# Four-layer graph network on one core: layer 1's blocks, the token order, and the inputs of layers 0 and 2

## The chip, the core and the metric

The kernel runs on one core of a Trainium2 chip. A core has five engines that run side by side, each through its own list of instructions in order: TensorE (PE) multiplies matrices, VectorE (DVE) and ScalarE (ACT) work element by element, GpSimd (POOL) does the same and also issues the indirect transfers (gathers and scatters by index), and SyncE (SP) issues most other transfers. They wait for each other through semaphores. Matmul results land in PSUM, which has eight banks; everything else is in SBUF (on chip) or in DRAM. The metric is the device time of one execution in microseconds (us); lower is better.

## What is computed

The input is 3125 nodes with 256 features each, in fp32, and 50,000 edges. Four layers follow. Each normalises the rows, adds a graph part and a mixing part, and adds an expert or feed-forward part. What matters here:

```python
# every layer (layer 3 differs in details)
xn = _layernorm(x)
x = x + gnn(xn, edges) + mix(xn)
x = x + ffn(_layernorm(x))
# layer 0's ffn: 8 experts, all applied to all nodes, weighted with softmax(x @ Wr + br)
# layer 1's ffn: a shared expert (256 -> 1024 -> 256, gelu) for all nodes, and
#   8 routed experts (256 -> 1024 -> 256, gelu): each node takes its two best
# layer 3's graph part runs a scan over the nodes in this order:
perm = jnp.argsort(deg + deg_noise, stable=True)
```

`deg` counts a node's outgoing edges and `deg_noise` is an input, so layer 3's order depends on the inputs alone and can be found at any earlier time.

## The kernel before

The nodes lie in 25 tiles of 125 partitions (P = 125, NT = 25); `GROUPS` are six groups of four tiles and one of one. The residual X stays in SBUF through all four layers. The program text gives each operation once, in Python loops; a scheduler decides at build time in which order each engine's list holds them, from their dependences and from the pools (a pool is a region of SBUF or PSUM; a tile of a later pool may lie where an earlier pool's tiles lay, and then has to wait for them). At run time every engine keeps to its list.

Helpers. `evac` (L74) copies a PSUM result to SBUF, by VectorE (L78) and ScalarE (L80) in turn. `turn` (L144) transposes tiles on TensorE into the layout that matmuls need. `hidden` (L540) and `outward` (L553) are the two matrix products of an expert. `halves` (L778) splits a transfer in two. `layer_input` (L521) goes through the seven groups: for each tile the statistics (bn_stats L125, bn_aggr L126), a few small operations for 1/sqrt(variance), the normalised tile XN (L138), and its transposes into XNT.

Layer 0's experts, `l0_ffn` (L783): the layer's input; then `probabilities` (the router: 100 matmuls of eight columns, and a softmax); then for each of eight experts and seven groups two hidden products and one outward product, whose results VectorE adds into X with the node's weight (L825). In expert 1 the folded output biases are added tile by tile (`expert_bias`). One pool of seven PSUM banks serves all of this, and the layer's input has a pool of four banks (`li_ps`) that is opened and closed inside `layer_input`. Just before it comes layer 0's graph aggregation (agg, L759), 1250 matmuls with the adjacency read from DRAM, with X accumulated at its end.

Layer 1 starts in `layer1` (L1548), which first fills 8000 rows of DRAM (`f_rows`, 8 MB) with zeros, in eight transfers of 1 MB on the queues of SyncE and ScalarE in turn (`blank`, L1537). Its experts, `l1_ffn` (L1392): the input; the router; `l1_route`, which sorts the node and expert pairs so that each expert's nodes fill blocks of 250 rows (BLK), with `put[k]` the row of each node's k-th pair, `share[k]` its weight, and `owner[b]` the expert of block b. MAXB = 32 blocks is the number that can never be exceeded: 2 x 3125 pairs and up to 249 empty rows for each of eight experts. GpSimd scatters the nodes into `f_rows`, the shared expert runs, and then the loop over all 32 blocks. `load(b)` (L1436) reads a block's rows and its expert's 2 MB of weights on SyncE's queue, one block ahead, with three buffers. The block is turned (xbt), goes through `hidden` (hb, eight chunks, gelu on ScalarE) and `outward`, its two halves are copied to yb by VectorE and ScalarE in turn, and two transfers on ScalarE's queue write them to `f_out` in DRAM (L780, L781).

After the loop comes `l3_order` (L1872), which finds layer 3's order: `places` (L1684) spreads the keys of all nodes into every partition (25 transposes on TensorE, seven evacuations to place_row), and then counts on VectorE, tile by tile, how many keys are below each node's own (L1702): for tile i one tally over the i tiles before it (place_t), one over its own tile (place_e), and one over the tiles from i on (place_t), 74 in all. They read place_row and a mask of ones. A reduction (L1708) and a cast (L1881) give the order.

Then 50 gathers (`gather`, L2083, GpSimd) fetch each node's two rows from `f_out` to yg (six buffers, in the pool f1_k of the block loop), and VectorE adds each to X with its share (L1469). Layer 2 opens with `layer_input` (`layer2`, L1751), whose XN and XNT lie where layer 1's pools lay; the projection of layer 2's graph part puts h2 (h22, al22) beside h in the pool g2_h.

Of the kernel before, what the change touches and what calls it, by code (L numbers as in the profile page):

```python
# [12 lines left out]
F32 = mybir.dt.float32  # L13
BF16 = mybir.dt.bfloat16
I32 = mybir.dt.int32
# [3 lines left out]
PSUM = bass.MemoryType.PSUM  # L19
# [33 lines left out]
FMAX = 3.4028234663852886e38  # L53
BLK = 2 * P
MAXB = (2 * N + 8 * (BLK - 1)) // BLK
CAP = 489
GROUPS = [(g, min(4, NT - g)) for g in range(0, NT, 4)]
COLUMNS = [(0, 7), (7, 6), (13, 6), (19, 6)]
# [2 lines left out]
class Net:  # L61
# [456 lines left out]

    def layer_input(self, pool=None, xn=None, xnt=None):  # L521

        if pool is not None:
            xn = pool.tile([P, NT, D], F32, name="XN")
            xnt = pool.tile([128, KC, N], F32, name="XNT")
        with self.pool("li", 2) as wp, self.pool("li_ps", 4, PSUM) as pp:
            for g, n in GROUPS:
                self.normed(wp, xn[:, g:g + n, :], self.X[:, g:g + n, :], n, 1e-5, "li")
                self.turn(pp, xnt[:, :, g * P:(g + n) * P], xn[:, g:g + n, :], n)
        return xn, xnt  # L530
# [249 lines left out]
        queue.dma_start(out[:EVEN], in_[:EVEN])  # L780
        queue.dma_start(out[EVEN:], in_[EVEN:])  # L781

    def l0_ffn(self):  # L783
        nc = self.nc
        pre = "L0_ffn_"
        with ExitStack() as es:
            sp = es.enter_context(self.pool("f0"))
            xn, xnt = self.layer_input(sp)
            wp = es.enter_context(self.pool("f0_w", 2))
            kp = es.enter_context(self.pool("f0_k", 2))  # L790
            pp = es.enter_context(self.pool("f0_ps", 7, PSUM))
            wr = self.weight(sp, pre + "Wr")
            br = self.rows(sp, pre + "br")
            prob = self.probabilities(sp, pp, xnt, wr, br)
            more = self.expert_bias(sp, pp, prob, pre + "bo")
            scale, bias = [], []
            for k in ("1", "2"):
                b, g, be, m, v = (self.cols(sp, pre + t + k) for t in ("b", "g", "be", "m", "v"))
                s = sp.tile(list(v.shape), F32, name="bn_s" + k)
                nc.vector.tensor_scalar(v, v, 1e-3, None, op0=ALU.add)  # L800
                self.rsqrt(sp, s, v, "bn" + k)
                nc.vector.tensor_mul(s, s, g)
                nc.vector.tensor_sub(b, b, m)
                nc.vector.tensor_mul(b, b, s)
                nc.vector.tensor_add(b, b, be)
                scale.append(s)
                bias.append(b)
            mp = es.enter_context(self.pool("f0_m", 2))
            for e in range(8):
                w1 = self.weight(wp, pre + "W1", view=self.ins[pre + "W1"][e])  # L810
                w2 = self.weight(wp, pre + "W2", view=self.ins[pre + "W2"][e])
                wo = self.weight(wp, pre + "Wo", view=self.ins[pre + "Wo"][e])
                ce = slice(e * KC, (e + 1) * KC)
                for g, n in GROUPS:
                    w = n * P
                    h1 = kp.tile([128, KC, 4 * P], F32, name="h1")
                    h2 = kp.tile([128, KC, 4 * P], F32, name="h2")
                    self.hidden(pp, h1[:, :, :w], w1, [xnt[:, c, g * P:g * P + w] for c in range(KC)],
                                KC, AF.Relu, bias[0][:, ce], scale[0][:, ce])
                    self.hidden(pp, h2[:, :, :w], w2, [h1[:, c, :w] for c in range(KC)],  # L820
                                KC, AF.Relu, bias[1][:, ce], scale[1][:, ce])

                    def use(j, ps):
                        x = self.X[:, g + j, :]
                        nc.vector.scalar_tensor_tensor(x, ps, prob[:, g + j, e:e + 1], x,  # L825
                                                       op0=ALU.mult, op1=ALU.add)
                    self.outward(pp, h2, wo, KC, n, use)
                    if e == 1:
                        for _ in range(n):
                            next(more)  # L830
                    if g % 8 == 0 and e * 4 + g // 8 < NT:
                        self.mask_row(mp, e * 4 + g // 8)

    def layer0(self):
        with self.under_way:
            fill = self.fill_adjacency()
            for k, _ in enumerate(self.l0_mix(self.xnt0)):
                for _ in range(2 if k % 4 else 1):
                    next(fill, None)
            self.through(fill)  # L840
            self.sums.close()
            with self.pool("g0_h") as hp:
                h = self.l0_gnn_project(hp, self.xnt0)
                left = self.nc.values_load(self.left[0:1, 0:1], min_val=0, max_val=1)
                with self.tc.If(left > 0):
                    self.any_adjacency()
                self.l0_gnn(h)
        self.l0_ffn()

# [540 lines left out]
    def l1_ffn(self):  # L1392

        nc = self.nc
        pre = "L1_ffn_"
        with ExitStack() as es:
            sp = es.enter_context(self.pool("f1"))
            put = [sp.tile([P, NT], I32, name=f"put{k}") for k in range(2)]  # L1400
            share = [sp.tile([P, NT], F32, name=f"share{k}") for k in range(2)]
            owner = sp.tile([P, MAXB], I32, name="owner")
            rows = self.rows1
            out = self.dram.tile([MAXB * BLK, D], F32, name="f1_out")
            wp = es.enter_context(self.pool("f1_w", 3))
            kp = es.enter_context(self.pool("f1_k", 2))
            with ExitStack() as es2:
# [8 lines left out]
                nc.gpsimd.tensor_add(self.X, self.X, b2s[:, None, :].to_broadcast([P, NT, D]))  # L1416
                prob = self.probabilities(ip, pp, xnt, wr)
                rank = self.ranks(ip, prob)
                self.l1_route(ip, pp, prob, rank, put, share, owner)
                self.apart([self.scatter(rows, put[k][:, i:i + 1], xn[:, i, :]) for i in range(NT)  # L1420
                            for k in range(2)], "all pairs' rows differ")
                more = self.expert_bias(ip, pp, prob, pre + "b2p")
# [23 lines left out]
                nc.sync.dma_start(b1, self.ins[pre + "b1p"][bass.ds(e, 1)].rearrange("o p f -> p (o f)"))  # L1446
                return x, w1, w2, b1

            ahead = load(0)
            for b in range(MAXB):  # L1450
                (x, w1, w2, b1), ahead = ahead, load(b + 1) if b + 1 < MAXB else None
                xt = kp.tile([128, KC, BLK], F32, name="xbt")
                self.turn(pp, xt, x, 2)
                h = kp.tile([128, 8, BLK], F32, name="hb")
                self.hidden(pp, h, w1, [xt[:, c, :] for c in range(KC)], 8, AF.Gelu, b1)
                y = kp.tile([P, 2, D], F32, name="yb")

                def keep(j, ps):
                    self.evac(y[:, j, :], ps)
                self.outward(pp, h, w2, 8, 2, keep)  # L1460
                self.halves(nc.scalar, out[b * BLK:(b + 1) * BLK, :].rearrange("(j p) d -> p j d", p=P), y)

            self.l3_order(pp)
            for i in range(NT):
                for k in range(2):
                    y = kp.tile([P, D], F32, name="yg", bufs=6)
                    self.gather(y, out, put[k][:, i:i + 1])
                    x = self.X[:, i, :]
                    nc.vector.scalar_tensor_tensor(x, y, share[k][:, i:i + 1], x, op0=ALU.mult, op1=ALU.add)  # L1469

    def l1_route(self, pool, psum, prob, rank, put, share, owner):


        nc = self.nc
# [44 lines left out]
        nc.vector.tensor_reduce(number, past, axis=AX.X, op=ALU.add)  # L1519
        nc.vector.tensor_scalar(number, number, 7.0, None, op0=ALU.min)  # L1520
        nc.vector.tensor_copy(owner, number)

        nc.vector.tensor_add(off[:, :NT, :], off[:, :NT, :],
                             within[:P, :NT * 8].rearrange("p (i e) -> p i e", e=8))
# [9 lines left out]
            nc.vector.tensor_mul(t, prob, chosen)  # L1534
            nc.vector.tensor_reduce(share[k], t, axis=AX.X, op=ALU.add)

    def blank(self, rows, count):  # L1537

        nc = self.nc
        with self.pool("blank") as zp:  # L1540
            width = count * D // 128
            zero = zp.tile([128, width // 8], F32, name="zero")
            nc.gpsimd.memset(zero, 0.0)
            zv = rows.rearrange("r d -> (r d)").rearrange("(b p f) -> b p f", b=8, p=128)
            for b in range(8):
                (nc.sync, nc.scalar)[b % 2].dma_start(zv[b], zero)

    def layer1(self):  # L1548
        self.rows1 = self.dram.tile([MAXB * BLK, D], F32, name="f1_rows")
        self.blank(self.rows1, MAXB * BLK)  # L1550
        with self.pool("g1_h") as hp:
            with self.pool("in1") as ip:
                xn, xnt = self.layer_input(ip)
# [119 lines left out]
                nc.gpsimd.tensor_add(self.X[:, g:g + n, :], self.X[:, g:g + n, :], y[:, :n, :])  # L1673
        return h

    def l2_gnn_project(self, pool, xnt):
        h2 = pool.tile([P, NT, 1, D + 1], F32, name="h22")
        al2 = pool.tile([P, NT, 2], F32, name="al22")
        return self.gat_project(pool, xnt, "L2_gnn_", "W1", 4, ("a_src1", "a_dst1"), "g2") + (h2, al2)

    def l2_gnn(self, h):
# [67 lines left out]
                self.outward(pp, h, w2, 8, n, use)  # L1749

    def layer2(self):  # L1751
        with self.pool("g2_h") as hp:
            with self.pool("in2") as ip:
                xn, xnt = self.layer_input(ip)
                h = self.l2_mix(xn, xnt, lambda: self.l2_gnn_project(hp, xnt))
            self.l2_gnn(h)
        self.l2_ffn()

# [690 lines left out]
```

## Time and profile before

| what | us |
|---|---|
| median of 3 runs | 7255.4 |
| the runs | 7255.02, 7258.82, 7255.40 |
| the profiled execution | 7258.78 |
| its span, first to last instruction | 7257.0 |
| TensorE busy | 6018.7 (83%) |
| VectorE busy | 3847.7 (53%) |
| ScalarE busy | 1528.9 (21%) |
| GpSimd busy | 980.6 (14%) |
| layer 1's block loop: 1024 + 1024 matmuls | 227.5 + 226.2 |

The mean granted clock of TensorE is 0.889 of full speed (PEclk in the windows is the same figure for a stretch of time). Times in the rows of the profile count from the start of the span. A row of the groups has the line of the kernel, the engine, the operation, output<-inputs by name, the shapes and how often; then the busy time, the mean duration and the idle time before, with the event that ended it. A row of the order of time has start and duration in us, and in brackets how long the engine stood idle before it and what released it. The busy shares are means over stages of very different kinds, so a stage has to be read by its own window.

### The profile page before, as it was taken

Reading aid. Unit: us, or ns where it says so; the run is one execution under the profiler, and the core shown is the slowest. Engines: PE = TensorE matmul, PEld = TensorE weight load, DVE = VectorE, ACT = ScalarE, POOL = GpSimd, SP = SyncE. Lnnn points to the kernel's source line nnn. Section 1 sums busy time; section 2 is a strip of 40 time slices with the busy share of each in tenths; the row PEclk is TensorE's granted clock in tenths of the full one; section 3 lists DMA queues with packets and bytes.
Section 4 is the critical chain, followed back from the end, with each engine's and each line's share of the span. In section 5 each row is a group of like instructions: output and inputs, shape, how many; then the busy total and the mean of one; then the engine's idle time right before and its main releaser. Section 6 shows DMA issues by size and latency. Waiting matters only on the chain. (4 is left out here: it accounts for less than half of the span.)

```text
span 7257.0 us, 79169 instructions
## 1 busy us (share of the span) xinstructions
PE 6018.7 (83%) x29841; PEld 4048.7 (56%) x29841; DVE 3847.7 (53%) x7861; ACT 1528.9 (21%) x3255; POOL 980.6 (14%) x730
## 2 busy tenths in 40 slices
PE   6887999995999897999816998988788879985584
PEld 5555874554999786678714344875444343333452
DVE  7643223128666644110276887456377878776504
ACT  1333012331001100222213011001366640012110
POOL 0000000004000011300141000111244440002302
PEclk8877998997999998989957998989799979997697
DMA  2523457101221142245310222421300012220131
GB/s 65 105 50 65 136 160 235 35 5 61 60 60 56 51 133 84 75 135 179 117 36 23 79 75 66 136 73 31 56 12 17 9 43 82 69 59 21 39 127 56
DMA packets 407126, 540.56 MB, mean 74 GB/s; under 512 B 116440, under 2 KB 292187, under 8 KB 402939
## 3 DMA queue, kind: packets, MB, share of 16 engines
q1 hardware_dynamic: 355276, 462.70, 23.1%
q10 hardware_dynamic: 24664, 45.08, 2.0%
q0 software_dynamic: 26752, 27.19, 1.4%
q8 instruction: 248, 4.06, 0.2%
q14 instruction: 186, 1.52, 0.1%
HBM read 425.19 MB, written 109.43 MB: 74 GB/s over the span
## 5 line engine op out<-in xcount | busy, mean ns | idle before, releaser
L1109 DVE SCALAR_TENSOR_TENSOR t<-rows,over,a 125x625 f32<-125x625 f32 x750 | 621.9, 871 | 411.6 <-PE acc L1114 410.9
L1175 DVE SCALAR_TENSOR_TENSOR t<-rows,over,a 125x750 f32<-125x750 f32 (+1 forms) x800 | 795.4, 1045 | 57.6 <-PE acc L1189 53.1
L1180 PE MATMUL acc<-t,g_h 125*64 125x375 f32 (+1 forms) x3200 | 626.0, 501 | 12.8 <-DVE t L1175 12.8
L1114 PE MATMUL acc<-g_h,t 125*125 125x129 f32 x5000 | 568.5, 276 | 1.3 <-DVE t L1109 1.1
L1114 PE MATMUL acc<-h,t 125*125 125x257 f32 x2500 | 557.7, 386 | 13.8 <-DVE share_r L1221 7.1
L1114 PEld LDWEIGHTS acc<-g_h,t 125*125 125x125 f32 x5000 | 565.8, 190 | 2.7 <-DVE t L1109 2.7
L1114 PEld LDWEIGHTS acc<-h,t 125*125 125x125 f32 x2500 | 474.9, 191 | 95.6 <-issue 9.4
L1180 PEld LDWEIGHTS acc<-t,g_h 125*64 125x64 f32 x3200 | 227.6, 137 | 356.2 <-issue 246.3
L1189 PE MATMUL acc<-t,g_h 125*32 125x375 f32 (+1 forms) x3200 | 377.1, 497 | 0.0
L2030 POOL TENSOR_TENSOR bx<-h,crow 128x500 f32<-128x500 f32 (+1 forms) x224 | 265.6, 1201 | 388.8 <-DVE h L2027 278.9
L149 PE MATMUL ps_turn<-ident,XN 125*128 125x125 f32 x350 | 76.7, 390 | 287.0 <-DVE XN L138 244.8
L825 DVE SCALAR_TENSOR_TENSOR X<-ps_out,prob,X 125x256 f32<-125x256 f32 x200 | 87.8, 479 | 397.6 <-PE ps_out L156 397.5
L759 PE MATMUL agg<-h,a 125*125 125x257 f32 x1250 | 278.6, 384 | 15.3 <-DMA a<-adj 9.1
L2036 PE MATMUL y<-bx,ident 128*128 128x500 f32 (+1 forms) x448 | 234.1, 633 | 48.2 <-POOL bx L2030 46.6
L759 PEld LDWEIGHTS agg<-h,a 125*125 125x125 f32 x1250 | 234.6, 189 | 59.4 <-issue 17.3
L2027 DVE TENSOR_TENSOR_SCAN h<-da,state,bx 128x500 f32<-128x500 f32 (+1 forms) x224 | 246.8, 1131 | 11.7 <-ACT da L2025 8.4
L78 DVE COPY yb<-ps_out 125x256 f32<-125x256 f32 x32 | 13.6, 424 | 446.6 <-issue 394.3
L1189 PEld LDWEIGHTS acc<-t,g_h 125*32 125x32 f32 x3200 | 104.2, 109 | 249.2 <-issue 248.4
L156 PE MATMUL ps_hidden<-xbt,w 128*128 128x250 f32 x1024 | 227.5, 380 | 14.5 <-DVE xbt L78 14.4
L551 ACT ACTIVATE h<-ps_hidden,L_ffn_b,bn_s 128x500 f32<-128x500 f32 (+1 forms) x224 | 160.7, 722 | 373.2 <-PE ps_hidden L156 365.6
L149 PEld LDWEIGHTS ps_turn<-ident,XN 125*128 125x128 f32 x350 | 60.2, 203 | 302.4 <-issue 263.7
L156 PE MATMUL ps_out<-w,hb 128*125 128x256 f32 x1024 | 226.2, 379 | 0.0
(723 smaller groups left out, 10048.3 us busy)
## 6 DMA issues: line engine op xcount, KB each, us to landing
a<-adj SPq DMA_DIRECT2D x500, 273.4 KB
a<-adj SPq DMA_DIRECT2D x150, 328.1 KB
arow<-adj SPq DMA_DIRECT2D x25, 1367.2 KB
adj<-block SPq DMA_DIRECT2D x22, 1531.2 KB
w<-in_L_ffn_W1p SPq DMA_DIRECT2D x32, 1024.0 KB
w<-in_L_ffn_W2p SPq DMA_DIRECT2D x32, 1024.0 KB
a<-adj SPq DMA_DIRECT2D x50, 382.8 KB
L_ffn_w<-in_L_ffn_w SPq DMA_DIRECT2D x18, 1024.0 KB
```

Source lines behind the costliest of these rows:

```text
L149: self.nc.tensor.transpose(ps[:, j * P:(j + 1) * P], x[:, j, c * 128:(c + 1) * 128], self.ident[:P, :P])
L156: self.nc.tensor.matmul(ps, lhsT[k], rhs[k], start=(k == 0), stop=(k == n - 1))
L551: self.nc.scalar.activation(out[:, f, :], ps[:, :nt], func, **kw)
L759: nc.tensor.matmul(acc[b][:P, :D + 1], a[:, b * P:(b + 1) * P], h[:, s, :], start=(s == 0), stop=(s == NT - 1))
L1109: nc.vector.scalar_tensor_tensor(t[:, hd, :], rows[:, hd, :], over[:, s, hd:hd + 1], a, op0=ALU.max, op1=ALU.mult)
L1114: nc.tensor.matmul(acc(b, hd), t[:, hd, b * P:(b + 1) * P], h[:, s, hd, :], start=(s == 0 and first), stop=(s == NT - 1), skip_group_check ...
L1175: nc.vector.scalar_tensor_tensor(t[hd][:, :w], rows[hd][:, :w], over[:, s, hd:hd + 1], a[:, :w], op0=ALU.max, op1=ALU.mult)
L1180: nc.tensor.matmul(acc[k][c][q * width:(q + 1) * width, :c1 - c0], h[:, s, 2 * k + q, :width], t[2 * k + q][:, c0:c1], start=(s == 0), sto ...
L1189: nc.tensor.matmul(acc[pairs][c][hd * 32:(hd + 1) * 32, :c1 - c0], h[:, s1, hd, width:].to_broadcast([P, 32]), t1[hd][:, c0:c1], start=(s1 ...
L2027: nc.vector.tensor_tensor_scan(h[:, :w], da[:, :w], bx[:, :w], state[:, c, s:s + 1], op0=ALU.mult, op1=ALU.add)
L2030: nc.gpsimd.tensor_mul(bx[:, :w], h[:, :w], crow[:, :w])
L2036: nc.tensor.matmul(acc[c][:, :w], self.ident, terms[c][:, :w], start=(s == 0), stop=(s == S - 1))
```

## The change

Layer 3's order is computed inside the block loop, after block 6. The loop runs over OFTEN = 29 blocks; the number of blocks that hold rows is kept in a tile `filled` by `l1_route`, every engine reads it into a register after block 28, and three more blocks stand in a branch that is entered when it is above 29. Their weights are loaded inside the branch. `layer1` now makes `f_out` too and fills its last 750 rows with zeros: one memset and four transfers of 192 KB each, after those of `f_rows`. The gathered rows yg get a pool of their own (f1_g, six buffers) opened before the block loop's pools, and layer 2 opens a pool g2_h2 for h2 below its others, in the place of yg's. Layer 0's experts get a PSUM pool of three banks (out_ps), opened in `layer0` before the aggregation; their input's transposes and their outward products use it, and the rest keeps five banks.

```diff
 FMAX = 3.4028234663852886e38
 BLK = 2 * P
 MAXB = (2 * N + 8 * (BLK - 1)) // BLK
+OFTEN = 29
 CAP = 489
 GROUPS = [(g, min(4, NT - g)) for g in range(0, NT, 4)]
 COLUMNS = [(0, 7), (7, 6), (13, 6), (19, 6)]
...
-    def layer_input(self, pool=None, xn=None, xnt=None):
+    def layer_input(self, pool=None, xn=None, xnt=None, pp=None):
         if pool is not None:
             xn = pool.tile([P, NT, D], F32, name="XN")
             xnt = pool.tile([128, KC, N], F32, name="XNT")
-        with self.pool("li", 2) as wp, self.pool("li_ps", 4, PSUM) as pp:
+        with self.pool("li", 2) as wp, ExitStack() as es:
+            pp = pp or es.enter_context(self.pool("li_ps", 4, PSUM))
             for g, n in GROUPS:
                 self.normed(wp, xn[:, g:g + n, :], self.X[:, g:g + n, :], n, 1e-5, "li")
                 self.turn(pp, xnt[:, :, g * P:(g + n) * P], xn[:, g:g + n, :], n)
...
         queue.dma_start(out[:EVEN], in_[:EVEN])
         queue.dma_start(out[EVEN:], in_[EVEN:])
-    def l0_ffn(self):
+    def l0_ffn(self, lp):
         nc = self.nc
         pre = "L0_ffn_"
         with ExitStack() as es:
             sp = es.enter_context(self.pool("f0"))
-            xn, xnt = self.layer_input(sp)
+            xn, xnt = self.layer_input(sp, pp=lp)
             wp = es.enter_context(self.pool("f0_w", 2))
             kp = es.enter_context(self.pool("f0_k", 2))
-            pp = es.enter_context(self.pool("f0_ps", 7, PSUM))
+            pp = es.enter_context(self.pool("f0_ps", 5, PSUM))
             wr = self.weight(sp, pre + "Wr")
             br = self.rows(sp, pre + "br")
             prob = self.probabilities(sp, pp, xnt, wr, br)
...
                         x = self.X[:, g + j, :]
                         nc.vector.scalar_tensor_tensor(x, ps, prob[:, g + j, e:e + 1], x,
                                                        op0=ALU.mult, op1=ALU.add)
-                    self.outward(pp, h2, wo, KC, n, use)
+                    self.outward(lp, h2, wo, KC, n, use)
                     if e == 1:
                         for _ in range(n):
                             next(more)
...
                         self.mask_row(mp, e * 4 + g // 8)
     def layer0(self):
+        over = ExitStack()
         with self.under_way:
             fill = self.fill_adjacency()
             for k, _ in enumerate(self.l0_mix(self.xnt0)):
...
                     next(fill, None)
             self.through(fill)
             self.sums.close()
+            lp = over.enter_context(self.pool("out_ps", 3, PSUM))
             with self.pool("g0_h") as hp:
                 h = self.l0_gnn_project(hp, self.xnt0)
                 left = self.nc.values_load(self.left[0:1, 0:1], min_val=0, max_val=1)
                 with self.tc.If(left > 0):
                     self.any_adjacency()
                 self.l0_gnn(h)
-        self.l0_ffn()
+        self.l0_ffn(lp)
+        over.close()
...
         nc = self.nc
         pre = "L1_ffn_"
         with ExitStack() as es:
...
             put = [sp.tile([P, NT], I32, name=f"put{k}") for k in range(2)]
             share = [sp.tile([P, NT], F32, name=f"share{k}") for k in range(2)]
             owner = sp.tile([P, MAXB], I32, name="owner")
+            filled = sp.tile([P, 1], I32, name="filled")
             rows = self.rows1
-            out = self.dram.tile([MAXB * BLK, D], F32, name="f1_out")
+            out = self.out1
+            gp = es.enter_context(self.pool("f1_g", 6))
             wp = es.enter_context(self.pool("f1_w", 3))
             kp = es.enter_context(self.pool("f1_k", 2))
             with ExitStack() as es2:
...
                 nc.gpsimd.tensor_add(self.X, self.X, b2s[:, None, :].to_broadcast([P, NT, D]))
                 prob = self.probabilities(ip, pp, xnt, wr)
                 rank = self.ranks(ip, prob)
-                self.l1_route(ip, pp, prob, rank, put, share, owner)
+                self.l1_route(ip, pp, prob, rank, put, share, owner, filled)
                 self.apart([self.scatter(rows, put[k][:, i:i + 1], xn[:, i, :]) for i in range(NT)
                             for k in range(2)], "all pairs' rows differ")
                 more = self.expert_bias(ip, pp, prob, pre + "b2p")
...
                 nc.sync.dma_start(b1, self.ins[pre + "b1p"][bass.ds(e, 1)].rearrange("o p f -> p (o f)"))
                 return x, w1, w2, b1
-            ahead = load(0)
-            for b in range(MAXB):
-                (x, w1, w2, b1), ahead = ahead, load(b + 1) if b + 1 < MAXB else None
+            def block(b, x, w1, w2, b1):
                 xt = kp.tile([128, KC, BLK], F32, name="xbt")
                 self.turn(pp, xt, x, 2)
                 h = kp.tile([128, 8, BLK], F32, name="hb")
...
                 self.outward(pp, h, w2, 8, 2, keep)
                 self.halves(nc.scalar, out[b * BLK:(b + 1) * BLK, :].rearrange("(j p) d -> p j d", p=P), y)
-            self.l3_order(pp)
+            ahead = load(0)
+            for b in range(OFTEN):
+                now, ahead = ahead, load(b + 1) if b + 1 < OFTEN else None
+                block(b, *now)
+                if b == 6:
+                    self.l3_order(pp)
+            total = nc.values_load(filled[0:1, 0:1], min_val=0, max_val=MAXB)
+            with self.tc.If(total > OFTEN):
+                for b in range(OFTEN, MAXB):
+                    block(b, *load(b))
             for i in range(NT):
                 for k in range(2):
-                    y = kp.tile([P, D], F32, name="yg", bufs=6)
+                    y = gp.tile([P, D], F32, name="yg")
                     self.gather(y, out, put[k][:, i:i + 1])
                     x = self.X[:, i, :]
                     nc.vector.scalar_tensor_tensor(x, y, share[k][:, i:i + 1], x, op0=ALU.mult, op1=ALU.add)
-    def l1_route(self, pool, psum, prob, rank, put, share, owner):
+    def l1_route(self, pool, psum, prob, rank, put, share, owner, filled):
         nc = self.nc
...
         nc.vector.tensor_reduce(number, past, axis=AX.X, op=ALU.add)
         nc.vector.tensor_scalar(number, number, 7.0, None, op0=ALU.min)
         nc.vector.tensor_copy(owner, number)
+        nc.vector.tensor_copy(filled, begin[:, 8:])
         nc.vector.tensor_add(off[:, :NT, :], off[:, :NT, :],
                              within[:P, :NT * 8].rearrange("p (i e) -> p i e", e=8))
...
             nc.vector.tensor_mul(t, prob, chosen)
             nc.vector.tensor_reduce(share[k], t, axis=AX.X, op=ALU.add)
-    def blank(self, rows, count):
+    def blank(self, rows, count, parts=8):
         nc = self.nc
         with self.pool("blank") as zp:
             width = count * D // 128
-            zero = zp.tile([128, width // 8], F32, name="zero")
+            zero = zp.tile([128, width // parts], F32, name="zero")
             nc.gpsimd.memset(zero, 0.0)
-            zv = rows.rearrange("r d -> (r d)").rearrange("(b p f) -> b p f", b=8, p=128)
-            for b in range(8):
+            zv = rows.rearrange("r d -> (r d)").rearrange("(b p f) -> b p f", b=parts, p=128)
+            for b in range(parts):
                 (nc.sync, nc.scalar)[b % 2].dma_start(zv[b], zero)
     def layer1(self):
         self.rows1 = self.dram.tile([MAXB * BLK, D], F32, name="f1_rows")
+        self.out1 = self.dram.tile([MAXB * BLK, D], F32, name="f1_out")
         self.blank(self.rows1, MAXB * BLK)
+        self.blank(self.out1[OFTEN * BLK:, :], (MAXB - OFTEN) * BLK, 4)
         with self.pool("g1_h") as hp:
             with self.pool("in1") as ip:
                 xn, xnt = self.layer_input(ip)
...
                 nc.gpsimd.tensor_add(self.X[:, g:g + n, :], self.X[:, g:g + n, :], y[:, :n, :])
         return h
-    def l2_gnn_project(self, pool, xnt):
-        h2 = pool.tile([P, NT, 1, D + 1], F32, name="h22")
-        al2 = pool.tile([P, NT, 2], F32, name="al22")
+    def l2_gnn_project(self, pool, low, xnt):
+        h2 = low.tile([P, NT, 1, D + 1], F32, name="h22")
+        al2 = low.tile([P, NT, 2], F32, name="al22")
         return self.gat_project(pool, xnt, "L2_gnn_", "W1", 4, ("a_src1", "a_dst1"), "g2") + (h2, al2)
     def l2_gnn(self, h):
...
                 self.outward(pp, h, w2, 8, n, use)
     def layer2(self):
-        with self.pool("g2_h") as hp:
+        with self.pool("g2_h2") as low, self.pool("g2_h") as hp:
             with self.pool("in2") as ip:
                 xn, xnt = self.layer_input(ip)
-                h = self.l2_mix(xn, xnt, lambda: self.l2_gnn_project(hp, xnt))
+                h = self.l2_mix(xn, xnt, lambda: self.l2_gnn_project(hp, low, xnt))
             self.l2_gnn(h)
         self.l2_ffn()
```

## The prediction

> **What bounds the kernel now.** I looked first at the span and clock (7257.0 us, 0.889), then at the busy times by window around the two layers that the change touches, then at VectorE's and GpSimd's instructions in order of time. The profiled execution took 7258.78 us, 3.4 more than the median 7255.4. I make the sum against 7258.8 and carry the difference over. 0.2% of the time is 14.5 us, about what a measurement can tell from no change.
>
> By window (columns: PE, PEld, DVE, ACT, POOL busy with counts, then PEclk, DMA share, GB/s):
> ```profile
> 1050.00:1640.00 590.00, 567.15 (x1777) 321.68 (x1775) 155.62 (x320) 164.25 (x238) 1.91 (x1) 0.96 0.35 106
> ...
> 3500.00:3600.00 100.00, 96.74 (x470) 84.34 (x468) 7.56 (x22) 28.70 (x66) 0.00 (x0) 1.00 0.34 110
> 3600.00:3680.00 80.00, 0.00 (x0) 0.00 (x0) 79.96 (x125) 0.50 (x2) 20.87 (x6) 0.52 0.04 10
> 3680.00:3765.00 85.00, 0.00 (x0) 0.00 (x0) 39.92 (x80) 1.28 (x1) 62.46 (x46) 0.50 0.26 67
> 3765.00:3850.00 85.00, 59.28 (x311) 47.67 (x312) 60.06 (x208) 45.56 (x155) 13.77 (x3) 0.86 0.04 10
> ```
> Layer 0's experts (first row) and layer 1's blocks (second) are bound by TensorE. Then 165 us follow with no matmul: first VectorE alone sets the end (79.96 of 80 us), then GpSimd. VectorE in order of time (start, us; some rows left out):
> ```profile
> 3582.07 0.42 DVE L78 COPY yb<-ps_out 125x256 f32<-125x256 f32 x1 [14.08 <-issue]
> ...
> 3596.90 0.42 DVE L78 COPY yb<-ps_out 125x256 f32<-125x256 f32 x1 [14.08 <-issue]
> 3597.29 0.68 DVE L78 COPY place_row<-ps_spread 125x500 f32<-125x500 f32 x1
> ...
> 3600.30 0.35 DVE L1702 SCALAR_TENSOR_TENSOR place_e<-place_row,key,earlier 125x125 f32<-125x125 f32 x1
> ...
> 3683.88 0.07 DVE L1702 DVE_READ_ACCUMULATOR place_t<-place_row,key,place 125x1 f32 x1
> ...
> 3762.84 0.48 DVE L1469 SCALAR_TENSOR_TENSOR X<-yg,share,X 125x256 f32<-125x256 f32 x1 [1.09 <-DMA yg<-f_out,put]
> ```
> A block costs 3596.90−3582.07 = 14.83 us, and VectorE works under 1 us of it. The order's tallies run 3597.29 to 3696.69, 99.4 us. From the last yb to the last X is 3597.32 to 3763.32, 166.0 us. GpSimd's gathers in that time:
> ```profile
> 3601.78 3.41 POOL L2083 DMA_INDIRECT yg<-f_out,put  x1 [482.58 <-issue]
> 3605.49 3.48 POOL L2083 DMA_INDIRECT yg<-f_out,put  x1 [0.30 <-issue]
> ...
> 3684.65 3.79 POOL L2083 DMA_INDIRECT yg<-f_out,put  x1 [60.47 <-DVE X L1469]
> ...
> 3750.95 1.22 POOL L2083 DMA_INDIRECT yg<-f_out,put  x1 [0.30 <-issue]
> ...
> 3758.68 1.21 POOL L2083 DMA_INDIRECT yg<-f_out,put  x1 [0.30 <-DVE X L1469]
> ```
> Six go out beside the tallies at 3.8 us apart, then six buffers are full until VectorE accumulates (60.47 us). Clear of the tallies, 39 steps from 3698.55 to 3758.68 are 1.542 us each.
>
> **The change part by part.**
>
> *Three blocks fewer.* Counting each expert's tokens with the given inputs (67, 564, 408, 999, 890, 1104, 1781, 437) and rounding each up to blocks of 250 gives 1+3+2+4+4+5+8+2 = 29, so the branch for total > 29 isn't entered: −3 × 14.83 = **−44.5 us**.
>
> *The order moved behind block 6.* "Beside the blocks" need not mean hidden: engines run in order. In the changed program as built, VectorE's list has yb(6), three place_e with the row copies, xbt(7), and then every tally up to the 125x500 of i=21 in one run, before yb(7) and xbt(8). TensorE can finish block 7 and then needs xbt(8). The same run lasted 3600.30 to 3683.95 above, 83.65 us. With yb(7), 0.40, two more tallies, 3.60, and xbt(8), 0.41, xbt(8) ends 88.1 us after xbt(7) began its wait for the run, where 14.83 is usual: a stall of 73.2. The row copies and place_e ahead of xbt(7) add the 3600.30−3597.29 = 3.0 of the row above: **76.3 us**. The 25 spreads and ScalarE's share of the copies lie within it; yb(7)'s writes on ScalarE's queue wait too, but nobody reads them before the gathers. The rest of the tallies (four more, the reduction, the cast; about 8 us) falls in block 8's 14.83 us, where VectorE has 14.08 idle; uncovered it would cost those 8. TensorE restarts at half clock: at layer 2's start PEclk is 0.50 and 0.55 in 3765–3775 and 1.00 from 3775, with work from 3770.57, so some 4.4 us at half speed, **+2.2**. Sum +78.5.
>
> *The gathers without tallies beside them.* A first gather 4.5 us after the last yb (3601.78 against 3597.32), 49 steps of 1.542 = 75.6, and 4.64 from the last gather's start to the last X: 84.7 us for 166.0, **−81.3**. On this the skill has a rule: Trainium Architecture — The Big Picture, section "What this means for kernel authors", says VectorE and GpSimd share a port pair by an exclusive lock. The rows agree as to the tallies (3.41 to 3.79 us beside them, 1.21 clear), and the rule speaks against a part of this change: layer 2's input is now to run beside the gathers. By the rule at its worst all 49 steps take 3.8; by the nearest row, layer 3's 25 scatters, they stay near 1.5:
> ```profile
> L2087 POOL DMA_INDIRECT xs<-XN,order x25: 1187/1188/1475, 5053.3 to 5093.2; - x25
> ```
> There VectorE did this same layer input 23.15 of 41.0 us. I take the row, 1.542.
>
> *The branch.* The engines load `total` and jump. The nearest row is layer 0's untaken branch: SyncE issues at 716.02 and next at 719.09, 2.7 us lost. Advanced Engine Details and Errata, "Control Flow Timing", has 0.1 us for a compare-and-branch; the row includes loading the register. SyncE and GpSimd arrive before block 28 ends, so only part can show: 0 to 4, I take **+1.5**.
>
> *Layer 2's input beside the gathers.* Before, 29.2 us pass from the last X to the last XN at 3792.5. As built, 11 of 25 statistics, 7 of 25 XN and the first groups' small operations come before the last X: 11 × 0.39 + 7 × 0.40 + ten of 0.15 + one copy of 0.6 = **−9** (−5 to −13). Filling the rows later cannot help: the remaining groups need the last X.
>
> *Layer 0's input with three banks of its own.* From the last agg at 1009.33 to the first hidden at 1043.30: 7.0 idle, 50 turns 7.65, 100 router matmuls 19.0. As built, 23 turns go inside the agg stream (at 0.153 each 3.5 us, a cost), 17 into the idle, and the router starts on the first groups: net −2 to −6.5, I take −4.5. In expert 1 TensorE waits 14.9 us for folded weights (10.6 on VectorE, 4.3 on ScalarE); with out's banks apart other matmuls can go between, −4 (0 to −8). Fifty groups come 10.45 apart, 10.2 without stalls: −3.5 (+3 to −10; five banks for hidden instead of seven could also cost). Sum **−12** (0 to −25).
>
> *Blanking the last 750 rows.* Four writes of 192 KB; GpSimd's memset waits for the first blanks (GpSimd was held so to 1656.23), and ScalarE's issue of two stands ahead of its copies at 1653.46 and 1655.65 for layer 1's input: **+3** (0 to 5). If SyncE and ScalarE were clear it were nothing.
>
> Sum: −44.5 + 78.5 − 81.3 + 1.5 − 9 − 12 + 3 = −63.8; 7258.8 becomes 7195, the median **7192** (−0.9%). Order and gathers together give only −1.3: the 99 us tail of VectorE becomes a stall of 76 amid the blocks. The late thing after it is the gather chain.
>
> **Rivals.**
> 1. *The order is hidden after all*: VectorE's tallies interleave with yb and xbt. 14.08 us idle in each of 22 blocks would take them. Against it the list as built. 7192 − 76 − 2 = 7114. Chance 0.03.
> 2. *The branch is taken.* Expert 3 has 999 of 1000 tokens that fit; two tokens decided otherwise by rounding give 30 blocks. +44.5, and up to 18 for weights that are not fetched ahead (2 MB at the blocks' 178 GB/s is 11.8, plus some 6 landing and jump): 7236 to 7254, no change. Chance 0.06.
> 3. *The gathers stay slow* (the slower side): the lock above held by layer 2's statistics and XN for all 49 steps; 49 × (3.79−1.54) = +110 gives 7302. It decides from 3.15 us a step, 49 × 1.61 = 79 making it over 0.2% slower. For it, the 3.8 beside the tallies; against it, 1.5 beside the same input in layer 3, and that only 11 of 25 statistics stand there. Chance 0.04.
> 4. *Layer 0 gains nothing or loses 3, the rest as forecast*: 7204 to 7207; or all its ends are good: 7179. Both in the likeliest's range.
>
> **How the numbers follow.** Likeliest, 0.87: 7192, its own range 7165 (every part at its good end: L0 −13 more, input −4, blank −3, branch −1.5, stall −5) to 7222 (+12, +4, +2, +2.5, and 10 for the uncovered tallies or a longer stall). Range 7160 to 7225, which leaves out rivals 1 to 3, 0.13. Faster 0.91 (the likeliest, rival 1, a little of 2), same 0.05, slower 0.04.
>
> **What would show it.** A hole of 70 to 80 us in TensorE behind block 7 with VectorE full; 29 block cadences of 14.83 besides; no tallies after the last yb and gathers 1.5 apart at once; 85 to 88 us from the last yb to the last X; last X to last XN near 20; agg to hidden in layer 0 under 32. A block cadence merely longer by 3 to 4 us over 22 blocks would mean rival 1; gathers over 2.8 apart, rival 3; matmuls of three further blocks, rival 2.

## The result and the profile after

The changed kernel took 7180.16 us in the median of 4 runs (7176.12 to 7182.51); the kernel before took 7257.11 beside it. The ratio is 0.9886 with an interval of 0.9866 to 0.9907: faster by 1.1%. Forecast were 7192 and a range of 7160 to 7225. The profiled execution has a span of 7179.0 us (before 7257.0, so −78.0) and a clock of 0.884.

I cut both traces at the same instructions and put the forecast beside the differences. Times are those of the profiled executions, in us. Here ps_h is the first product of layer 1's graph part, and qkv that of layer 2's mixing part.

| stretch | before | after | difference | forecast |
|---|---|---|---|---|
| start to layer 0's first agg | 724.5 | 730.6 | +6.1 | 0 |
| first agg to layer 0's first hidden | 318.8 | 316.1 | −2.7 | −4.5 |
| layer 0's experts, to layer 1's first turn | 590.0 | 558.8 | −31.2 | −7.5 |
| layer 1's input, to its first ps_h | 33.8 | 36.1 | +2.3 | +3 |
| to the first hidden of block 0 | 1453.5 | 1454.2 | +0.7 | 0 |
| the blocks, to the last yb | 476.8 | 504.8 | +28.0 | −44.5 + 78.5 |
| last yb to last X | 165.4 | 84.9 | −80.5 | −79.8 |
| last X to layer 2's first qkv | 47.9 | 43.0 | −4.9 | −9 |
| the rest | 3446.3 | 3450.5 | +4.2 | 0 |

By window, columns as in the same view of before (us, then busy time of PE, PEld, DVE, ACT and POOL with counts, PEclk, DMA share, GB/s):

```profile
1050.00:1640.00 590.00, 555.14 (x1816) 328.40 (x1814) 180.12 (x402) 169.34 (x251) 5.45 (x5) 0.96 0.39 119
...
3200.00:3300.00 100.00, 29.52 (x135) 24.79 (x134) 98.80 (x158) 9.87 (x22) 0.00 (x0) 0.64 0.14 42
3300.00:3600.00 300.00, 293.94 (x1392) 255.24 (x1390) 15.22 (x41) 87.52 (x201) 0.00 (x0) 1.00 0.49 158
3600.00:3690.00 90.00, 16.09 (x57) 10.96 (x57) 36.98 (x112) 9.72 (x32) 62.75 (x52) 0.55 0.31 75
```

The 165 us without a matmul have split in two: a stretch inside the blocks where VectorE is full (98.80 of 100 us) and TensorE has 29.52, and a tail of 85 us that belongs to GpSimd (62.75 of 90). TensorE in order of time at the first of them, in the changed kernel:

```profile
3211.84 7.07 PE L157 MATMUL ps_out<-w,hb 128*125 128x256 f32 x32
3218.75 0.59 PE L150 MATMUL ps_turn<-ident,xb 125*128 125x125 f32 x4
3219.64 2.38 PE L157 MATMUL ps_hidden<-xbt,w 128*128 128x250 f32 x10 [0.30 <-ACT xbt L81]
3288.67 1.20 PE L157 MATMUL ps_hidden<-xbt,w 128*128 128x250 f32 x2 [66.66 <-DVE yb L79]
3292.53 7.44 PE L157 MATMUL ps_hidden<-xbt,w 128*128 128x250 f32 x20 [2.66 <-DVE xbt L79]
```

This is the forecast hole: block 7 finishes (ps_out), block 8 is turned, and hidden waits 66.66 us for yb (a copy out of PSUM) and 2.66 for xbt, both behind the tallies on VectorE. The ten matmuls at 3219.64 go ahead with the half of xbt that ScalarE copies. VectorE's list there:

```profile
3171.39 0.42 DVE L79 COPY yb<-ps_out 125x256 f32<-125x256 f32 x1 [14.08 <-issue]
...
3204.92 3.47 DVE L1720 SCALAR_TENSOR_TENSOR place_t<-place_row,key,place 125x3125 f32<-125x3125 f32 x1
...
3288.20 0.42 DVE L79 COPY yb<-ps_out 125x256 f32<-125x256 f32 x1
...
3292.06 0.42 DVE L79 COPY xbt<-ps_turn 128x250 f32<-128x250 f32 x1
...
3307.32 0.42 DVE L79 COPY yb<-ps_out 125x256 f32<-125x256 f32 x1 [7.17 <-ACT yb L81]
...
3321.99 0.42 DVE L79 COPY yb<-ps_out 125x256 f32<-125x256 f32 x1 [13.92 <-ACT yb L81]
```

From the first place_t to yb(7) are 83.3 us with nothing but tallies (place_t and place_e) between. GpSimd's gathers now start clear of them:

```profile
3605.24 1.24 POOL L2101 DMA_INDIRECT yg<-f_out,put  x1 [510.79 <-SPq L1476]
3606.79 1.22 POOL L2101 DMA_INDIRECT yg<-f_out,put  x1 [0.30 <-issue]
3608.32 1.21 POOL L2101 DMA_INDIRECT yg<-f_out,put  x1 [0.30 <-issue]
```

### The profile page after: what moved, and what is told of

It is laid out like the page before. It is cut to its first block, busy times and chain, and to the rows that moved or that the text cites. A ratio compares the mean times of both kernels' runs of the same rounds, so it can differ in the third digit from the quotient of the medians.

```text
span 7179.0 us, 78723 instructions
## 1 busy us (share of the span) xinstructions
PE 5977.8 (83%) x29637; PEld 4020.4 (56%) x29637; DVE 3846.0 (54%) x7856; ACT 1515.4 (21%) x3225; POOL 961.0 (13%) x731
## 5 line engine op out<-in xcount | busy, mean ns | idle before, releaser
L157 PE MATMUL ps_hidden<-xbt,w 128*128 128x250 f32 x928 | 210.1, 384 | 79.3 <-DVE yb L79 66.7
L157 PEld LDWEIGHTS ps_hidden<-xbt,w 128*128 128x128 f32 x928 | 177.3, 194 | 107.6 <-DVE yb L79 67.0
L157 PE MATMUL ps_out<-w,hb 128*125 128x256 f32 x928 | 205.0, 379 | 0.0
```

Of the source, the lines that this page charges most:

```text
L157: self.nc.tensor.matmul(ps, lhsT[k], rhs[k], start=(k == 0), stop=(k == n - 1))
```

## The experiments

Each kernel is the changed one with one edit. Medians are given with that of the kernel before on the same chip, since that differs by up to 12 us from one set of runs to another; the stretches come from the kernel's own trace.

**The order back behind the blocks.**

```diff
-                if b == 6:
-                    self.l3_order(pp)
...
                     block(b, *load(b))
+            self.l3_order(pp)
```

> The changed kernel with the token order back behind the blocks, all else changed. Mine (the order's tallies stop the blocks wherever they stand as one run on VectorE): the hole of 73 us behind block 7 goes, and the tail from the last yb to the last X goes from 85 back to about 166, so +81 -73 = +8, near 7188 us. Rival (the move really hides most of the order, and the hole has another cause): the hole stays and the tail comes back, near 7261. The first gathers, beside the tallies again, take 3.4 to 3.8 us each by both.

Measured: 7191.22 (before 7263.27, so −72; the changed kernel's own was −77). The blocks take 432.2 us and the tail 170.7, together 13 more than the changed kernel's 504.8 + 84.9, where 8 were expected. The hole is gone from the blocks, so the order made it; and the gathers beside the tallies are slow again, once the first of the long tallies (place_t) has begun at 3538.52:

```profile
3537.88 1.21 POOL L2100 DMA_INDIRECT yg<-f_out,put  x1 [0.30 <-issue]
3539.39 3.69 POOL L2100 DMA_INDIRECT yg<-f_out,put  x1 [0.30 <-issue]
3543.38 3.50 POOL L2100 DMA_INDIRECT yg<-f_out,put  x1 [0.30 <-issue]
```

The tail is 5 us longer than before's 165.4. Here the order stands behind the branch (L1474): its spreads on TensorE start 3.23 us after the last product and take 4.60, where they took 2.89 directly behind it in the kernel before.

```profile
3519.90 7.07 PE L157 MATMUL ps_out<-w,hb 128*125 128x256 f32 x32
3530.19 4.60 PE L165 MATMUL ps_spread<-ident,key 125*125 125x125 f32 x25 [3.23 <-ACTq L1474]
```

**The order handed out among the blocks.** `places` becomes a generator that yields after each tile, and the loop advances it. (Shown in part; what is left is advanced to its end after the loop.) As built, VectorE's list has three or four tiles' tallies between the copies of two blocks:

```diff
+            order = self.l3_order(pp)
...
-                if b == 6:
-                    self.l3_order(pp)
+                if b >= 2:
+                    next(order, None)
```

> The changed kernel with the same 74 tallies handed out one tile per block from block 2 on, so that VectorE's list has yb and xbt between them (as built, three or four tiles, 11 to 14 us, stand between two blocks' copies). Mine: the 14.08 us that VectorE has idle in a block take them, the hole of 69 us goes but for the spreads (3) and some 0.5 to 1 us a block over eight blocks: 7180 - 65 = 7115 us (7108 to 7122). Rival (the hole is not the list's order but the tallies themselves slowing the blocks, through PSUM or SBUF): the same 70 us spread over the eight blocks, near 7180.

Measured: 7097.05 (before 7263.27; ratio 0.9775, interval 0.9759 to 0.9792). The blocks take 431.0 us where they took 504.8, the tail is unchanged (84.5). VectorE's and TensorE's rows of this kernel:

```profile
3151.17 0.42 DVE L79 COPY yb<-ps_out 125x256 f32<-125x256 f32 x1
3151.51 0.41 DVE L79 COPY xbt<-ps_turn 128x250 f32<-128x250 f32 x1
3151.84 0.73 DVE L1725 SCALAR_TENSOR_TENSOR place_t<-place_row,key,place 125x500 f32<-125x500 f32 x1
...
3166.78 0.41 DVE L79 COPY yb<-ps_out 125x256 f32<-125x256 f32 x1
```

```profile
3143.29 7.07 PE L157 MATMUL ps_out<-w,hb 128*125 128x256 f32 x32
3150.19 0.59 PE L150 MATMUL ps_turn<-ident,xb 125*128 125x125 f32 x4
3151.09 7.06 PE L157 MATMUL ps_hidden<-xbt,w 128*128 128x250 f32 x32 [0.30 <-ACT xbt L81]
3157.99 7.07 PE L157 MATMUL ps_out<-w,hb 128*125 128x256 f32 x32
3164.90 0.59 PE L150 MATMUL ps_turn<-ident,xb 125*128 125x125 f32 x4
```

VectorE is as busy with the same tallies, but yb and xbt stand between them, and TensorE goes from block to block with 0.30 us of waiting. The tallies do not slow the blocks; the list's order did. Expected were 7115 and a gain of 65. The stage gained 73.8; I had allowed 4 to 8 us of small stalls, and there are none: 432.2 without any order, less 0.16 for each of the 25 blocks after the swap of the copies (told below), plus 2.9 for the spreads on TensorE, is 431.1. What the total has beyond the stage is looked at with the last two runs. The portions are of some 15 us, as long as a block, so the copies come a little late (yb at 3166.78, 15.61 after the last); the buffers take that up.

**Layer 0's banks as before, seven and then eight shared.**

```diff
-            xn, xnt = self.layer_input(sp, pp=lp)
+            xn, xnt = self.layer_input(sp)
...
-            pp = es.enter_context(self.pool("f0_ps", 5, PSUM))
+            pp = es.enter_context(self.pool("f0_ps", 7, PSUM))
...
-                    self.outward(lp, h2, wo, KC, n, use)
+                    self.outward(pp, h2, wo, KC, n, use)
...
-            lp = over.enter_context(self.pool("out_ps", 3, PSUM))
+            lp = None
```

> The changed kernel with layer 0's experts as before: seven banks shared by all, the input's own four banks opened and closed first. If the banks are worth what the two traces differ by in layer 0 (31 us in the experts, less 3.4 at the front): 7180 + 28 = 7208. If they are worth the 12 that I forecast and the rest is scatter between executions: 7192. The experts from the first hidden to the last outward: 589 us by the first, 566 by the second.

The second kernel has 8 in place of 7.

> As the kernel with seven shared banks, but eight. If the eighth bank is what layer 0's experts gained (before had seven, now five and three): near 7180 to 7185, the experts at 558 to 565 us. If it is that outward's matmuls have banks of their own, so that the list may run hidden of the next group ahead: near 7205, the experts at 585 to 589.

Measured: 7205.27 with seven and 7205.71 with eight (before 7263.27), so both are 19 worse than the changed kernel, by their distances from before. From the last agg to the last X of layer 0's experts they take 625.3 and 623.4 us; before took 623.4 and the changed kernel 589.0 and, in its second profile (below), 592.3. The stage is the cleaner measure, since it leaves out what differs elsewhere: 31 to 36 us. Part of what differs can be seen: from the last product of layer 1's graph aggregation (acc) to the first scatter of its experts, these two kernels take 84.2 and 83.2 us, and the changed kernel 89.3 and 89.0 with the same operations in the same order in each engine's list; before took 87.4. The cause of this is open. The eighth bank is worth nothing; that outward has its own is what counts. TensorE in the kernel with eight shared banks, and then in the changed one:

```profile
1382.73 3.72 PE L157 MATMUL ps_out<-L_ffn_Wo,h 128*125 128x256 f32 x16
1386.29 3.52 PE L157 MATMUL ps_hidden<-XNT,L_ffn_W 128*128 128x500 f32 x8
1389.64 3.52 PE L157 MATMUL ps_hidden<-h,L_ffn_W 128*128 128x500 f32 x8
1393.18 3.72 PE L157 MATMUL ps_out<-L_ffn_Wo,h 128*125 128x256 f32 x16
```

```profile
1371.03 3.52 PE L157 MATMUL ps_hidden<-h,L_ffn_W 128*128 128x500 f32 x8
1374.38 1.00 PE L157 MATMUL ps_hidden<-XNT,L_ffn_W 128*128 128x500 f32 x2
1375.22 3.62 PE L157 MATMUL ps_out<-L_ffn_Wo,h 128*125 128x256 f32 x16
1378.67 2.68 PE L157 MATMUL ps_hidden<-XNT,L_ffn_W 128*128 128x500 f32 x6
```

With shared banks the list is hidden, hidden, outward, and a product waits a little for ScalarE's relu of the one before: the eight matmuls of ps_hidden<-XNT at 1386.29 hand over after 3.35 us, those of ps_hidden<-h at 1389.64 after 3.54. Outward starts at 1393.18, just behind the first of the two relus of ScalarE's row at 1392.36 (each some 0.77 us):

```profile
1392.36 1.61 ACT L553 ACTIVATE h<-ps_hidden,L_ffn_b,bn_s 128x500 f32<-128x500 f32 x2 [1.75 <-PE ps_hidden L157]
```

With own banks the first two matmuls of the next group stand ahead of outward and fill that time.

**The layer's input with banks of its own, outward still apart.**

```diff
-            xn, xnt = self.layer_input(sp, pp=lp)
+            xn, xnt = self.layer_input(sp)
```

> The changed kernel, in which outward keeps its three banks but the layer's input has four banks of its own again, opened behind the aggregation, so that no turn goes inside it. Mine: the gain of 31 us in the experts stays, and the front (last agg to first hidden) changes by -3 to +7: 7178 to 7187. Rival (the early turns are part of the experts' gain): 7195 or more.

Measured: 7174.90 (before 7254.18, −79). From the last agg to the last X of layer 0: 596.6 us. So outward's banks are worth 623.4 − 596.6 = 27, and the early turns 4 to 8 (589.0 and 592.3 in two profiles of the changed kernel). The total does not show that second part: this kernel, too, takes only 83.1 us from acc to layer 1's scatters, in place of 89. Whether that hangs together with the early turns is not shown.

**All 32 blocks in the loop.** OFTEN = 32, and the branch, its register load and the zeros are left out.

> The changed kernel with all 32 blocks in the loop, no branch and no zeros for the end of f_out. Mine: three blocks of 14.83 us are 44.5; less the branch (0 to 3) and the zeros' 2.3: 7220 to 7225. Rival (the empty blocks cost less than a cadence): below 7215.

Measured: 7204.54 (before 7254.18, −50), 27 above the changed kernel by the distances from before, where 40 was expected. The stretches do give it: blocks 548.7 against 504.8 (+43.9, for 44.5 forecast), the tail 83.0 against 84.9, layer 1's input 33.4 against 36.1. The missing 13 us lie in stretches with the same instructions in both (last section), so this total cannot price three blocks and the trace can.

**No branch.**

```diff
-            total = nc.values_load(filled[0:1, 0:1], min_val=0, max_val=MAXB)
-            with self.tc.If(total > OFTEN):
-                for b in range(OFTEN, MAXB):
-                    block(b, *load(b))
```

> The changed kernel without the branch and the register load ahead of it: 29 blocks whatever the counts are, which leaves the three further blocks' work out. Mine: the branch cost at most 2 us beside the gathers' start: 7178 to 7181. Rival (it costs the 2.7 us of layer 0's branch on the path, or more): 7175 to 7177.

Measured: 7172.60 (before 7254.18, −82, so 5 better than the changed kernel by the distances). Last yb to last X is 83.0 where the changed kernel has 84.9 and 84.9 in two profiles: the branch costs 1.9 us there. How much of it is left later is not shown: from the last yb to layer 2's first qkv it is 127.0 against 127.9 and 128.0. The other 3 are no larger than the scatter.

**The gathered rows and layer 2's tiles as before.**

```diff
-            gp = es.enter_context(self.pool("f1_g", 6))
...
-                    y = gp.tile([P, D], F32, name="yg")
+                    y = kp.tile([P, D], F32, name="yg", bufs=6)
...
-        with self.pool("g2_h2") as low, self.pool("g2_h") as hp:
+        with self.pool("g2_h") as hp:
...
-                h = self.l2_mix(xn, xnt, lambda: self.l2_gnn_project(hp, low, xnt))
+                h = self.l2_mix(xn, xnt, lambda: self.l2_gnn_project(hp, hp, xnt))
```

> The changed kernel with the gathered rows back in the block loop's pool and layer 2's tiles as before, so that layer 2's input starts after the last X. By the two traces last X to last XN takes 29 us again where it takes 23.5: 7185 to 7186 us. Rival (the 5.4 us are given back later in layer 2 or 3): 7180. My forecast's 9 us would give 7189.

Measured: 7178.45 (before 7254.18, −76; 1 worse). The last X to the first qkv is 48.5 us, against 43.0 and 43.1 with the change: 5.4 are gained there (the other kernels with this change and the order in the loop have 41.5 to 44.1). From qkv on no give-back is visible beyond the scatter, and the total is too coarse to settle whether all 5 arrive at the end.

**The changed kernel and the interleaved order once more, side by side.**

> The changed kernel once more, beside the next one, so that the two are compared on one chip with more runs. Layer 0's start (first agg at 720.9 to 737.3 us in the profiles so far), the stretch from layer 0's experts to layer 1's scatters (1272 to 1283) and layer 3's scan (1772 to 1778) differed between executions of programs that have the same instructions there. If that is scatter between executions, this run moves inside those bounds; if it belongs to the changed program, they come out as in its first profile (730.6, 1283.1, 1777.3).

> The interleaved order once more. By the stages it should be 74 us faster than the changed kernel (504.8 - 431.0 in the blocks); the medians of two different jobs make it 89. If the other 15 us are scatter: 71 to 78 us under the run beside it. If the interleaved program has a gain elsewhere: 85 or more.

Measured: 7178.56 and 7101.03 (before 7266.30; the ratios 0.9877, interval 0.9862 to 0.9892, and 0.9773, 0.9759 to 0.9786). They lie 77.5 apart, inside what the stage gives (74) with its scatter, so the 15 us of the first comparison were none of the interleaving. The blocks are 505.0 and 431.1 us. The stretches of the two new traces move inside the earlier bounds, though the first agg, at 729.9 and 730.4, did not come back to before's 724.5. But all twelve traces together have it from 720.9 to 737.3, and the interleaved program alone at 720.9 and 730.4, so I read the table's +6.1 as scatter and not as a price of the change.

## Why the prediction held, point by point

- *Blocks.* Three fewer at 14.83 each: 548.7 − 504.8 = 43.9 for 44.5, and 44.6 between before's 476.8 and the 432.2 of the kernel with the order behind the blocks.
- *The order as a stall amid the blocks.* Forecast 78.5. The loop took 504.8, and 432.2 without the order, so 72.6. Two terms were off. After the order the cadence is 14.67, not 14.83 (yb at 3307.32 and 3321.99): the order's seven evacuations, an odd number, swapped which engine copies which half, and hidden now waits 0.30 us for ScalarE's half of xbt (the row at 3219.64 above) instead of 0.47 for VectorE's, as it still does in the kernel with the order behind the blocks:

```profile
3186.60 7.03 PE L157 MATMUL ps_hidden<-xbt,w 128*128 128x250 f32 x32 [0.47 <-DVE xbt L79]
```

Over 20 blocks that is −3.2. I had taken the swap to change nothing. And TensorE did ten matmuls of hidden(8), 2.4 us, ahead of the hole.
- *Gathers.* 84.9 us from yb to X for 84.7 + 1.5. The nearest row, layer 3's scatters at 1.5 a step, was the right one: the part of layer 2's input that runs beside the gathers did not slow them (1.21 us in the median and 1.43 at most, against 3.4 to 3.8 beside the tallies).
- *The branch.* 1.9 for 1.5.
- *Layer 2's input.* The term of −9 was mis-sized: 5.4. The built list did have 11 of 25 statistics ahead of the last X. But what follows is not VectorE alone. In the changed kernel it stands idle for ScalarE's square root (li_s, at 3694.95), an engine that the sum had left out. ScalarE's list has copies of layer 2's first products (ps_h) ahead of it, and these wait for TensorE:

```profile
3692.15 0.37 ACT L886 COPY g_h<-ps_h 125x256 f32<-125x256 f32 x1 [1.74 <-PE ps_h L157]
3694.68 0.37 ACT L886 COPY g_h<-ps_h 125x256 f32<-125x256 f32 x1 [1.72 <-PE ps_h L157]
3694.95 0.21 ACT L112 ACTIVATE li_s<-li_ve 125x4 f32<-125x4 f32 x1
3695.19 0.18 DVE L114 RECIPROCAL li_r<-li_s 125x4 f32<-125x4 f32 x1 [3.29 <-ACT li_s L112]
```

- *Layer 0.* The term of −12 (0 to −25) was the one most mis-sized, and outside its own range: 34, and 31 by the second profile of the changed kernel. I had the 0.29 us a group in sight (10.45 against 10.16 measured now) and booked a quarter of it, 3.5; it came whole. At the front, the 23 turns inside the aggregation made it 0.3 us longer in the first profile and 0.7 in the second, not the 3.5 booked. An expert has six full groups and one of a single tile, where 3.66 becomes 3.13: 2.27 an expert, 15.9 over seven. The eighth, expert 1 with the folded biases, fell from 118.5 to 102.9 us (from one single-tile group to the next), 15.6 for the 4 booked. TensorE's waits there, before and after:

```profile
PE ps_eb L676 <- DVE wt L78: 10.6, 13, 2.4
PE ps_eb L676 <- ACT wt L80: 4.3, 11, 0.4
...
PE ps_eb L678 <- DVE wt L79: 5.6, 7, 1.4
PE ps_eb L678 <- ACT wt L81: 3.2, 8, 0.4
```

They fell from 14.9 to 8.8, so 6 of the 15.6. In the window 1110 to 1200 the granted clock is 0.92 where it was 0.83, and, as an estimate, 0.09 of 90 us is 8, about the rest. The second profile of the changed kernel speaks for that too: its waits are the same 8.8, its clock in this window is 0.90, and expert 1 takes 105.6. No experiment sets the clock, so this part stays argued.
- *Zeros for f_out.* +2.3 for +3: first turn to first ps_h takes 36.1 and, without the zeros, 33.4.

The rivals: layer 0 gained more than the good end of rival 4, VectorE's tallies did not interleave by themselves, the trace has matmuls for 29 blocks and no more, and no gather took over 1.43 us.

The mechanism was right for the large terms: order and gathers together were to give −1.3, and 432.2 + 165.4 became 504.8 + 84.9, −7.9. It was incomplete for layer 2's input, where ScalarE was missing, and in layer 0 for expert 1. Sizes were off by 22 us in layer 0's banks and 6 in the stall, both towards faster, and by 4 the other way in layer 2's input; stretches that the change does not touch came out some 10 slower in this profile (+6.1 and +4.2 in the table). That the total missed by only 12 is in part luck: those 10 took back nearly half of what layer 0 gave beyond its term.

## What to carry to other kernels

"Beside" is a matter of the list, not of the place in the program: 99 us of VectorE work that fit into its idle time cost 73 when the list held them as one run, and nothing beyond 2.9 us of spreads on TensorE when it held them in portions of some 15 us with the copies between. So read the built order, hand work out in pieces no longer than one turn of the loop, and count waits of 0.2 us between products: here they were worth their full number once a separate set of banks let the next product start.

## What the runs showed that was not expected

Swapping which of two engines copies which half changed the blocks' cadence by 0.16 us (14.83 to 14.67): the first consumer waits 0.30 us for ScalarE's copy where it waited 0.47 for VectorE's.

An order of hidden, hidden, outward with full banks shows almost no waiting in TensorE's rows (3 us over the whole of layer 0 outside the biases), and yet 0.29 us in each full group could be gained (10.45 against 10.16); the time was inside the rows, which run to a modelled end.

Stretches that the change does not touch differ between the traces: 720.9 to 737.3 us to the first agg, 1272.0 to 1283.1 from layer 0's experts to layer 1's scatters (2.3 of it the zeros, where they are written, and 5 to 6 the shorter way to the scatters in the three kernels whose layer 0 input is not in outward's banks), 1772.3 to 1777.7 in layer 3's scan. In two of them the time goes with the granted clock. Layer 0's experts, from the first hidden to the last outward, take 557.4 to 557.6 us at a clock of 0.98 in four traces and 560.6 at 0.97 in four others, with the same 1771 matmuls in the same order. Layer 1's graph aggregation takes from 1004.9 us at 0.97 (all 32 blocks) to 1012.5 at 0.96 (the kernel before). Differences of totals under some 10 us said nothing here. A stage repeated within 2 in the blocks (503.3 to 505.0) and within 3 in layer 0's experts.
